# Finer load and store transfers, spread-out second statistics and shared buffers in a diagonal-LSTM and quantum-circuit kernel

## The chip, the cores and the metric

The kernel runs on one core of a Trainium2 chip. The metric is the device time of one execution in microseconds, the median of several runs. The core has five engines with queues of their own: PE (TensorE, matrix products; PEld is its weight load), DVE (VectorE), ACT (ScalarE), POOL (GpSimd) and SP (SyncE, which here only starts DMA transfers). Sixteen DMA engines move data between HBM and the on-chip SBUF, which all transfers share.

## The reference, cut to what matters

The input is 16 images of 128 channels and 64 x 64 pixels (33.5 MB in fp32). Layer 0 normalises, runs an LSTM along the diagonals of each image, and adds the result to its input. Layer 1 normalises that sum and applies, at every pixel, a small simulated quantum circuit, and adds again.

```python
def _gn(v, G=32, eps=1e-5):
    g = v.reshape(B_, G, C_ // G, H_, W_)
    m = jnp.mean(g, axis=(2, 3, 4), keepdims=True)
    s = jnp.var(g, axis=(2, 3, 4), keepdims=True)
    return ((g - m) / jnp.sqrt(s + eps)).reshape(v.shape)
...
x = x + _L0_conv_ref(_gn(x), L0_conv_w_is, L0_conv_b_is, L0_conv_w_ss, L0_conv_b_ss)
x = x + _L1_conv_ref(_gn(x), L1_conv_pre_w, L1_conv_pre_b, L1_conv_q_weights, L1_conv_post_w, L1_conv_post_b)
```

Each `_gn` needs the mean and the variance of a whole group (4 channels of one image, all pixels) before any pixel of layer 1 can be computed. The second `_gn` is therefore a barrier: its statistics are complete only after the last diagonal of layer 0.

## The kernel before, in words

**Stage 1, loading (0 to about 107 us).** All 16 images stream in. 40 of an image's 64 rows go into a resident buffer, `ring` (`rows(b)`, L230: for image 0 five pieces of 256 KB, for the others one piece of 1 MB and one of 256 KB). The other 24 rows are loaded only for statistics into rotating buffers (`behind(b)`, L239, three pieces of 256 KB, seven buffers). DVE takes `bn_stats` of every 128x512 piece (L263) in the order: ring rows of image b+1, then the rest of image b, then `bn_aggr` (L266). SP issues the loads in that same order. Beside this PE, ACT and POOL run 33 small recurrence steps (`inv_step`, L177 to L188), and `keep` (L332) issues products whose result nobody reads. After the last image come the group mean (`group_mean`, L137), the variance (L403 to L409) and `inverse_root` (L144 to L148), which gives `rstd1`; then POOL normalises the first diagonals (L546 to L556) and PE makes the first gates (L565).

**Stage 2, the scan (about 107 to 1290 us).** `NSTEP` = 160 diagonal steps. PE multiplies the hidden state (L694) and the next input (L565), ACT applies the gate functions (L713, L767), DVE forms the cell and hidden states (L757 to L776), POOL normalises the diagonal two steps ahead and adds the new hidden state onto the ring (`residual`, L599). Rows come finished in 16 groups of four rows (g = 0 to 15); `residual` appends the 16 images of a finished group to `waiting`, and in every step `statistics(n)` takes 4 or 6 of them with `bn_stats` over 128x256 (L651). After group 9 (`FIRST` = 10) a first sum is made (`early_sums`). The first 24 rows are written out to a DRAM scratch tensor, `low` (L605), and the rows that were left behind in stage 1 are loaded in their place (L655).

**The turn (1290 to 1303 us).** After the loop: `residual` of the last step, the `bn_stats` still waiting, then five DVE passes over the statistics of the last six groups (L619 to L631), the group sums on PE (L810), the variance (L811 to L815), `inverse_root`, and from `rstd2` and `mean2` the per-image weights `w_image` (L823) and offsets `b_image` (L832, with a product on PE, L831).

**Stage 3, the circuit (1303 to 1445 us).** Per image b: `angles` (theta, L865, 16 matmul records per image in the profile), `sines` (ACT L879, DVE L881 and L882, ACT L885), `squares` (PE L893, ACT L905), `outputs` (PE L911, in two halves of four 128x512 tiles) and `finish` (DVE L928: eight additions of 128x512 per image, result written over x1). Three of the eight chunks of an image lie in `low` and are loaded back by POOL (`load`, L854, 256 KB each, 14 buffers); the other five are in the ring. Stores: each low chunk alone (L930, 256 KB), and the ring rows by halves (L933: one chunk in the first half, four chunks as 1 MB in the second). A low buffer is free for the next load when its store has landed. The order on PE is outputs(b, 0), squares(b+1), outputs(b, 1), angles(b+3), so an `angles` that waits for a load also holds back the outputs behind it. All stages lie in a manual order: each engine works through its instructions as the program emits them.

Of the kernel before, what the change touches and what calls it, by code (L numbers as in the profile page):

```python
# [16 lines left out]
P = 128  # L17
# [11 lines left out]
FIRST = 10  # L29
# [50 lines left out]
def kernel(  # L80
# [28 lines left out]
    NLOW = NH - RING  # L109
    low = dram.tile([NB, P, NLOW * NW], F32, name="low")  # L110

# [9 lines left out]
    NG2 = NH // 4  # L121
    w_theta = const.tile([P, 128], F32, name="w_theta")
# [28 lines left out]
    with ExitStack() as scan:  # L151
# [16 lines left out]

        def inv_step(j, pool):
# [28 lines left out]
        with ExitStack() as prep:  # L198
            pp = prep.enter_context(tc.tile_pool(name="prep", bufs=1))
            rest_pool = prep.enter_context(tc.tile_pool(name="rest", bufs=7))  # L200
# [6 lines left out]
            ws_n = [rest_pool.tile([P, 2, 2 * P], F32, name=f"ws_n{i}", tag="rest") for i in range(2)]  # L207
            sum_n = rest_pool.tile([P, 4, P], F32, name="sum_n", tag="rest")
            wx_n = rest_pool.tile([P, 4, P], F32, name="wx_n", tag="rest")
# [14 lines left out]
            pieces = [(1, 5), (0, 1)]  # L224
            rests = {}

            def rows(b):
                for k0, k1 in ((1, 2), (2, 3), (3, 4), (4, 5), (0, 1)) if b == 0 else pieces:
                    at = (2 * k0 * ROWS - AHEAD) * NW if k0 else SLOTS * NW
                    nc.sync.dma_start(  # L230
                        out=ring[:, 2 * k0 : 2 * k1, b, :],
                        in_=xv[b, :, at : at + (k1 - k0) * CHUNK].rearrange("c (k n) -> c k n", n=BLOCK),
                    )

            def behind(b):
                rests[b] = []
                for k in range(RING * NW, NH * NW, CHUNK):
                    rest = rest_pool.tile([P, CHUNK], F32, name=f"rest{b}_{k}", tag="rest")
                    nc.sync.dma_start(out=rest, in_=xv[b, :, k : k + CHUNK])  # L239
                    rests[b].append(rest)  # L240
# [88 lines left out]
            def keep(pool, tag, v):  # L329

                ps = pool.tile([P, v.shape[-1]], F32, name=nc.get_next_instruction_name(), tag=tag)
                nc.tensor.matmul(ps, lhsT=ident, rhs=v, start=True, stop=True)  # L332

# [28 lines left out]
            for b in range(NB):  # L362
                if b + 2 < NB:
                    rows(b + 2)
                if b + 1 < NB:
                    behind(b + 1)
                    for k in (1, 2, 3, 4, 0):
                        statistics(b + 1, k)
                for k in (5, 6, 7):
                    statistics(b, k)  # L370
                aggregated(b)
                while b < NB - 1 and done * (NB - 1) < EARLY * (b + 1):
# [5 lines left out]
                    done += 1  # L378
            prep_ps.close()
# [18 lines left out]
            for v in (ring[:, 2, NB - 1, :], rests[NB - 1][0], rests[NB - 1][1]):  # L398
                keep(ps_small, "small", v)
# [5 lines left out]
            nc.vector.tensor_add(var, var, mv1[:, :, 1])  # L405
            ps = ps_small.tile([P, NB], F32, name="gv1", tag="small")
            nc.tensor.matmul(ps, lhsT=group, rhs=var, start=True, stop=True)
            keep(ps_gate, "gate", wxT)
            nc.vector.tensor_scalar_add(var, ps, EPS)  # L409
# [73 lines left out]
        dst = [work.tile([P, 2, NC], F32, name=f"diff{i}") for i in range(2)]  # L483
        edge = work.tile([P, NW, NB], F32, name="edge")
# [97 lines left out]
        def differences(t, now, diff):  # L582
            a, b = columns(t)
            nc.vector.tensor_sub(diff[:, 1, a:b], now[:, 1, a:b], now[:, 0, a:b])
            if a == 0:
                above = edge[:, t - BAND, :] if BAND <= t < BAND + NW else none
                nc.gpsimd.tensor_sub(diff[:, 0, 0:NB], above, now[:, 0, 0:NB])
# [4 lines left out]
        def residual(t, new):  # L592
# [8 lines left out]
            for g in range(NG2):  # L601
                if t == 4 * g + 3 + (NW - 1 if 4 * g < SLOTS else BAND + NW - 1 - SLOTS):
                    waiting.extend((g, i) for i in range(NB))
# [7 lines left out]

        parts = stats.rearrange("p b g (h s) -> p b (g h) s", s=3)
        moments = small.tile([P, 2, NB], F32, name="moments", tag="moments")
        more = small.tile([P, 2, NB], F32, name="more", tag="moments")

        def squared(k0, k1):

            dev = parts[:, :, k0:k1, 1]
            nc.vector.tensor_mul(dev, dev, dev)  # L619
            yield  # L620
            nc.vector.scalar_tensor_tensor(
                dev, parts[:, :, k0:k1, 2], 2.0 / BLOCK, dev, ALU.mult, ALU.add
            )
            yield

        def less_mean(k0, k1):
            dev = parts[:, :, k0:k1, 1]
            nc.vector.tensor_sub(dev, dev, mean2.unsqueeze(2).to_broadcast([P, NB, k1 - k0]))

        def total(to, k0, k1):  # L630
            nc.vector.reduce_sum(to, parts[:, :, k0:k1, 1], axis=mybir.AxisListType.X)  # L631

        def early_sums():
            k = 2 * FIRST
            total(moments[:, 0], 0, k)
            yield
            group_mean(ps_small, moments[:, 0], mean2, 2, 1.0 / k)
            less_mean(0, k)
            yield
            total(moments[:, 0], 0, k)  # L640
            yield
            yield from squared(0, k)
            total(moments[:, 1], 0, k)
# [3 lines left out]
        def statistics(n):  # L647
            for _ in range(min(len(waiting), n)):
# [3 lines left out]
                if (g, i) == (FIRST - 1, NB - 1):  # L652
                    sums.append(early_sums())
                if i == NB - 1 and 4 * g < NLOW:
# [30 lines left out]
        def step(t, ps):  # L685
# [42 lines left out]
            for later in sums:  # L728
                next(later, None)
# [3 lines left out]
            if t + 2 < NSTEP:  # L733
                normalised(t + 2)
            both = {}
# [49 lines left out]
            if t in (2, 3):  # L785
                nc.vector.memset(dst[t % 2], 0.0)
            if SLOTS - 1 <= t < SLOTS - 1 + NW:
                nc.gpsimd.tensor_copy(edge[:, t - SLOTS + 1, :], one_slot(new, SLOTS - 1))  # L788
            return later

# [3 lines left out]
        with tc.manual_schedule():  # L794
# [5 lines left out]
            residual(NSTEP - 1, hst[NSTEP % 2])  # L800
            statistics(len(waiting))
            k, n = 2 * FIRST, 2 * NG2
            less_mean(k, n)
            total(more[:, 0], k, n)
            for _ in squared(k, n):
                pass
            total(more[:, 1], k, n)
            nc.vector.tensor_add(moments, moments, more)
            ps = ps_small.tile([P, 2, NB], F32, name="gm3", tag="small")
            nc.tensor.matmul(ps, lhsT=group, rhs=moments, start=True, stop=True)  # L810
            nc.vector.tensor_scalar_mul(moments, ps, 1.0 / n)  # L811
            var = small.tile([P, NB], F32, name="var2", tag="gn_var")
            nc.vector.tensor_mul(var, moments[:, 0], moments[:, 0])
            nc.vector.tensor_sub(var, moments[:, 1], var)
            nc.vector.tensor_scalar_add(var, var, EPS)  # L815
            inverse_root(small, var, rstd2, 2)
            nc.vector.tensor_add(mean2, mean2, moments[:, 0])

            warm = small.tile([P, 1], F32, name="warm", tag="inv_t")
            nc.scalar.activation(warm, shift, AF.Sin)  # L820


        nc.vector.tensor_mul(  # L823
            w_image[:, :, 16:32],
            w_theta[:, 0:16].unsqueeze(1).to_broadcast([P, NB, 16]),
            rstd2.unsqueeze(2).to_broadcast([P, NB, 16]),
        )
        mr = small.tile([P, NB], F32, name="mr", tag="gn_var")
        nc.vector.tensor_mul(mr, mean2, rstd2)
# [174 lines left out]
```

## Time and profile before

| what | us |
|---|---|
| median of 3 runs | 1448.32 (1445.94 to 1449.99) |
| the profiled execution, its own time | 1447.33 |
| its span | 1445.3 |
| PE busy | 1364.7 (94%) |
| DVE busy | 972.1 (67%) |
| POOL busy | 897.7 (62%) |
| ACT busy | 764.1 (53%) |

The time of the profiled execution is 2.0 us more than its span, the stretch from the first to the last instruction. The shares of the busy time are averages over three stages that have different limits, so they say little about the two ends of the program. The row of the DMA engines' busy share does say something: in 40 slices of 36 us it stands at 9 tenths or more in the first two, at 8 or 9 in the last four, at nearly nothing in most of the slices between, and at 1 to 4 tenths in slices 17 to 22, where finished rows go out and the rows left behind come in.

### The profile page before, as it was taken

The numbers are of one execution on the slowest core, as the hardware profiler recorded it, in microseconds if no ns is written. First come the engines' busy times: TensorE is split into PE (matmuls) and PEld (weight loads), VectorE is DVE, ScalarE is ACT, GpSimd is POOL, SyncE is SP. The second block draws the span as 40 slices with busy tenths as digits, with TensorE's granted clock in tenths as the row PEclk, the third lists the DMA queues.
The fourth block names the chain that finished last, engine by engine and source line by source line (L and its number), as shares of the span: only waits on it lengthen the run. The fifth ranks groups of instructions, "written<-read, shape, count | busy, mean of one in ns | idle before, by whom it ended". The sixth has DMA issues, their size and how long they took to land. (4 is left out here: it accounts for less than half of the span.)

```text
span 1445.3 us, 19732 instructions
## 1 busy us (share of the span) xinstructions
PE 1364.7 (94%) x5942; PEld 964.2 (67%) x5942; DVE 972.1 (67%) x2450; ACT 764.1 (53%) x1855; POOL 897.7 (62%) x1717
## 2 busy tenths in 40 slices
PE   6778999999999999999999999999999998868887
PEld 5648887776677766677766777667776787853222
DVE  6884566566665666887777765555555588776786
ACT  5645665555555555555555555555555565533231
POOL 4215777776677777788887776666766676622210
PEclk9999999999999999999999999999999999999997
DMA  9970000000000000133444000000000000008998
GB/s 327 362 267 2 1 1 1 1 0 1 1 0 1 1 0 1 59 117 122 131 134 134 6 0 1 1 1 1 1 1 0 1 1 1 1 1 284 347 361 288
DMA packets 86008, 107.00 MB, mean 74 GB/s; under 512 B 3936, under 2 KB 70528, under 8 KB 85904
## 3 DMA queue, kind: packets, MB, share of 16 engines
q1 hardware_dynamic: 80624, 92.29, 18.9%
q0 software_dynamic: 4048, 12.67, 2.6%
q8 instruction: 47, 0.77, 0.2%
q10 hardware_dynamic: 1232, 0.80, 0.2%
q14 instruction: 57, 0.47, 0.1%
HBM read 59.61 MB, written 46.14 MB: 73 GB/s over the span
## 5 line engine op out<-in xcount | busy, mean ns | idle before, releaser
L565 PE MATMUL ps<-xn,wxT 128*128 128x512 f32 (+18 forms) x1280 | 481.3, 519 | 1.5 <-POOL xn L556 0.9
L709 DVE TENSOR_TENSOR ps<-ps,both 128x256 f32<-128x256 f32 (+9 forms) x544 | 219.2, 408 | 318.0 <-PE ps L694 311.6
L713 ACT ACTIVATE ps<-ps,bias 128x512 f32<-128x512 f32 (+23 forms) x480 | 268.3, 581 | 254.2 <-DVE ps L709 217.8
L565 PEld LDWEIGHTS ps<-xn,wxT 128*128 128x128 f32 x1280 | 232.3, 192 | 174.9 <-issue 155.6
L739 ACT COPY both<-ps 128x256 f32<-128x256 f32 (+9 forms) x544 | 191.4, 355 | 179.9 <-PE ps L694 160.2
L694 PE MATMUL ps<-diff,w0T 128*128 128x256 f32 (+14 forms) x1088 | 283.3, 363 | 0.0
L694 PE MATMUL ps<-diff,w1T 128*128 128x256 f32 (+14 forms) x1088 | 283.3, 362 | 0.0
L599 POOL TENSOR_TENSOR ring<-ring,hst 128x256 f32<-128x256 f32 (+8 forms) x488 | 247.8, 539 | 24.4 <-DVE hst L776 24.4
L694 PEld LDWEIGHTS ps<-hst,wsT 128*128 128x128 f32 x1088 | 195.9, 190 | 87.7 <-DVE hst L776 39.1
L694 PE MATMUL ps<-hst,wsT 128*128 128x256 f32 (+14 forms) x1088 | 241.4, 365 | 7.6 <-DVE hst L776 6.2
L694 PEld LDWEIGHTS ps<-diff,w0T 128*128 128x128 f32 x1088 | 199.8, 190 | 21.0
L694 PEld LDWEIGHTS ps<-diff,w1T 128*128 128x128 f32 x1088 | 199.8, 190 | 21.0
L556 POOL TENSOR_TENSOR xn<-xn,rstd 128x512 f32<-128x512 f32 (+10 forms) x160 | 170.8, 1067 | 14.8 <-DVE rstd L148 2.3
L551 POOL TENSOR_TENSOR xn<-ring 128x256 f32<-128x256 f32 (+8 forms) x213 | 146.8, 699 | 0.0
L776 DVE TENSOR_TENSOR hst<-g,ps 128x256 f32<-128x256 f32 (+13 forms) x320 | 107.8, 368 | 46.6 <-ACT g L767 44.1
L546 POOL TENSOR_TENSOR xn<-ring,mean 128x16 f32<-128x16 f32 (+8 forms) x247 | 130.4, 537 | 11.4 <-DVE mean L138 10.4
L767 ACT ACTIVATE g<-cst 128x256 f32<-128x256 f32 (+20 forms) x320 | 102.9, 368 | 64.6 <-DVE cst L766 64.0
L590 POOL TENSOR_TENSOR diff<-hst 128x240 f32<-128x240 f32 (+9 forms) x136 | 102.9, 756 | 40.8 <-DVE hst L776 37.0
L788 POOL COPY edge<-hst 128x16 f32<-128x16 f32 x64 | 25.1, 392 | 134.2 <-DVE hst L776 134.2
L766 DVE TENSOR_TENSOR cst<-cst,ps 128x256 f32<-128x256 f32 (+20 forms) x320 | 104.5, 368 | 5.5
L763 DVE TENSOR_TENSOR ps<-ps,g 128x512 f32<-128x512 f32 (+20 forms) x160 | 95.0, 594 | 18.3 <-ACT g L713 17.2
L713 ACT ACTIVATE g<-ps,bias 128x512 f32<-128x512 f32 (+20 forms) x160 | 97.3, 608 | 11.0 <-PE ps L694 3.3
(309 smaller groups left out, 1209.4 us busy)
## 6 DMA issues: line engine op xcount, KB each, us to landing
out_dram<-ring SPq DMA_DIRECT2D x16, 1024.0 KB, 6.0
ring<-in_x_dram SPq DMA_DIRECT2D x15, 1024.0 KB, 10.1
rest<-in_x_dram SPq DMA_DIRECT2D x48, 256.0 KB, 7.8
low<-ring SPq DMA_DIRECT2D x6, 2048.0 KB, 7.6
ring<-in_x_dram SPq DMA_DIRECT2D x6, 2048.0 KB, 8.0
low<-low POOLq DMA_DIRECT2D x48, 256.0 KB, 5.9
out_dram<-low SPq DMA_DIRECT2D x48, 256.0 KB, 4.6
ring<-in_x_dram SPq DMA_DIRECT2D x20, 256.0 KB, 10.1
```

Of the source, the lines that this page charges most:

```text
L546: nc.gpsimd.tensor_sub(by_pairs(xn, 0, j, n), x0, over(mean1, n))
L551: nc.gpsimd.tensor_sub(by_pairs(xn, 1, j, n), lower, of)
L556: nc.gpsimd.tensor_mul(v, v, r)
L565: nc.tensor.matmul(ps[g][:, :, a:b], lhsT=wxT[:, g * 128 : (g + 1) * 128], rhs=xns[t % 2][:, :, a:b], start=t > 0, stop=True, skip_group_c ...
L590: nc.gpsimd.tensor_sub(diff[:, 0, a1:b], now[:, 1, a1 - NB : b - NB], now[:, 0, a1:b])
L599: nc.gpsimd.tensor_add(x1, x1, by_pairs(new, q, j, n))
L694: nc.tensor.matmul(out, lhsT=w[:, g * 128 : (g + 1) * 128], rhs=rhs, start=False, stop=True, skip_group_check=True,)
L709: nc.vector.tensor_add(v, v, both[g][:, a:b])
L713: nc.scalar.activation(to[:, :, a:w], ps[g][:, :, a:w], FUNC[g], bias=bias[:, g : g + 1])
L739: nc.scalar.copy(both[g][:, a:b], ps[g][:, 0, a:b])
L766: nc.vector.tensor_add(c[:, q], c[:, q], ig[:, q])
L776: nc.vector.tensor_mul(new[:, q, a:v], th[:, q, a:v], act[GO][:, q, a:v])
```

## The change

What it does, part by part:

- **Loads in stage 1.** Every image's ring rows come in five pieces of 256 KB. Four of the seven buffers of `behind` are now fixed tiles, `spare`, which also hold the raw weights before, and serve as `diff` and `edge` in the scan and as four of the 14 low buffers in stage 3. The recurrence steps of an iteration are emitted ahead of its loads.
- **First statistics.** `keep` takes `wsT` for its weights and the rest pieces of the last two images for its data, and two more `keep` products stand around the variance's group sum.
- **Second statistics.** `early_sums` follows after group 7 (`FIRST` = 8). For each of groups 8 to 14, POOL subtracts the early mean, squares, and adds to running sums (`late_sums`, four operations). The last four images of group 14 and the last five of group 15 aren't taken by `bn_stats` on DVE but by two activations each on ACT (`by_scalar`, Identity and Square with a sum along the row). At the end PE adds all parts in one accumulator (`add`), with five `keep` products among them.
- **The turn.** ACT's Sqrt table is loaded by a one-column activation ahead; `w_image` is written for image 0 first, the others after.
- **Low loads.** Chunks 0 to 3 are loaded by SP at step 152 into the spare tiles. Later loads are emitted after `finish(b, 0)` instead of at the head of the iteration.
- **Stores.** Every chunk is stored alone, 256 KB, right after its addition.

```diff
-FIRST = 10
+FIRST = 8
+LATE = 4
...
+    spare = [const.tile([P, CHUNK], F32, name=f"spare{i}") for i in range(4)]
...
+            ORDERED = (1, 2, 3, 4, 0)
...
             def rows(b):
-                for k0, k1 in ((1, 2), (2, 3), (3, 4), (4, 5), (0, 1)) if b == 0 else pieces:
+                for k in ORDERED:
...
-            for v in (ring[:, 2, NB - 1, :], rests[NB - 1][0], rests[NB - 1][1]):
-                keep(ps_small, "small", v)
+            for v in (rests[NB - 2][0], rests[NB - 2][2], rests[NB - 1][0]):
+                keep(ps_small, "small", v[:, 0 : 3 * P])
...
+            keep(ps_gate, "gate", wxT[:, 0 : 3 * P])
             ps = ps_small.tile([P, NB], F32, name="gv1", tag="small")
             nc.tensor.matmul(ps, lhsT=group, rhs=var, start=True, stop=True)
             keep(ps_gate, "gate", wxT)
+            keep(ps_gate, "gate", wxT[:, 0:P])
...
-                    waiting.extend((g, i) for i in range(NB))
+                    n = {NG2 - 2: NB - LATE, NG2 - 1: NB - LATE - 1}.get(g, NB)
+                    waiting.extend((g, i) for i in range(n))
...
+        def deviations(engine, g, n):
+            d = dev[:, :, 0:n]
+            m = mean2[:, 0:n].unsqueeze(2).to_broadcast([P, n, 2])
+            engine.tensor_sub(d[:, 0], parts[:, 0:n, 2 * g : 2 * g + 2, 1], m)
+            engine.tensor_mul(d[:, 1], d[:, 0], d[:, 0])
+
+        def late_sums(g, n):
+            deviations(nc.gpsimd, g, n)
+            v = added[:, :, 0:n]
+            nc.gpsimd.tensor_add(v, v, dev[:, :, 0:n])
+            v = inner[:, 0:n]
+            nc.gpsimd.tensor_add(v, v, parts[:, 0:n, 2 * g : 2 * g + 2, 2])
+            yield
+
+        def by_scalar(g, i):
+            x1 = ring[:, block(4 * g), i, :]
+            for k, f in enumerate((AF.Identity, AF.Square)):
+                to = work.tile([P, BLOCK], F32, name=f"none{g}_{i}_{k}", tag=f"both{k}")
+                nc.scalar.activation(
+                    to, x1, f, bias=less[:, i : i + 1], accum_out=sums_of[:, g % 2, k, i : i + 1]
+                )
...
+            if t >= NSTEP - LATE:
+                by_scalar(NG2 - 2, NB - NSTEP + t)
+            if t == NSTEP - 8:
+                for n in range(4):
+                    low_rows(nc.sync, n, spare[n])
...
+            warm = small.tile([P, 1], F32, name="warm", tag="inv_t")
+            nc.scalar.activation(warm, shift, AF.Sqrt)
             residual(NSTEP - 1, hst[NSTEP % 2])
...
+            g, n = NG2 - 1, NB - LATE - 1
+            for i in range(n, NB):
+                by_scalar(g, i)
...
+            add(ps, by_half, moments, True)
+            for h in range(2):
+                add(ps, by_half, added[:, :, :, h])
+                add(ps[:, 1], by_one, inner[:, :, h])
+            add(ps, by_one, sums_of[:, 0])
+            for _ in range(3):
+                keep(ps_gate, "gate", wxT)
             statistics(len(waiting))
-            k, n = 2 * FIRST, 2 * NG2
-            less_mean(k, n)
-            total(more[:, 0], k, n)
-            for _ in squared(k, n):
-                pass
-            total(more[:, 1], k, n)
-            nc.vector.tensor_add(moments, moments, more)
...
+            deviations(nc.vector, g, n)
+            for h in range(2):
+                add(ps[:, 1, 0:n], by_one, parts[:, 0:n, 2 * g + h, 2])
+            add(ps, by_one, sums_of[:, 1])
+            for h in range(2):
+                add(ps[:, :, 0:n], by_half, dev[:, :, 0:n, h])
...
+            nc.vector.tensor_copy(m, ps[:, 0])
+            nc.vector.scalar_tensor_tensor(var, m, -1.0, m, ALU.mult, ALU.mult)
+            nc.vector.scalar_tensor_tensor(var, var, EPS, ps[:, 1], ALU.add, ALU.add)
+            for _ in range(2):
+                keep(ps_gate, "gate", wxT)
             inverse_root(small, var, rstd2, 2)
...
+            image_weights(0, 1)
+            nc.vector.tensor_add(mean2, mean2, m)
+            mr = small.tile([P, NB], F32, name="mr", tag="gn_var")
+            nc.vector.tensor_mul(mr, mean2, rstd2)
+            image_weights(1, NB)
...
-    lowp = ctx.enter_context(tc.tile_pool(name="lowp", bufs=14))
+    lowp = ctx.enter_context(tc.tile_pool(name="lowp", bufs=10))
...
             nc.vector.scalar_tensor_tensor(x1, y, b_out, x1, ALU.add, ALU.add)
-            if k < NT:
-                nc.sync.dma_start(out=ov[b, :, k * CHUNK : (k + 1) * CHUNK], in_=x1)
-        for r0, r1 in (((NLOW, SLOTS),), ((SLOTS, NH),))[h]:
-            q = block(r0)
-            nc.sync.dma_start(
-                out=ov[b, :, r0 * NW : r1 * NW].rearrange("c (k n) -> c k n", n=BLOCK),
-                in_=ring[:, q : q + (r1 - r0) // ROWS, b, :],
-            )
+            o = ov[b, :, k * CHUNK : (k + 1) * CHUNK]
+            nc.sync.dma_start(out=o if k < NT else o.rearrange("c (k n) -> c k n", n=BLOCK), in_=x1)
...
-            if b + 4 < NB:
-                load(b + 4)
             po = outputs(b, 0)
             later = sines(b + 2) if 0 < b < NB - 2 else iter(())
             finish(b, 0, po)
+            for n in range(NBUF + NT * b, min(NBUF + NT * b + NT, NT * NB)):
+                load(n)
```

## The prediction

> **What bounds the kernel now.** I read the strip of 40 slices first. PE stands at 9 through the scan, and DMA at 8 or 9 in the first three and the last four slices: the scan belongs to PE, both ends to transfers, or to what starts and ends them. The change hardly touches PE's work in the scan, so the time must come from the ends. There I read three views: the timeline of stage 1's end, the timeline of the turn, and busy time by stretches.
>
> The end of stage 1 (start us, us, engine, line, operation, count, idle time before):
>
> ```profile
> 95.80 3.06 DVE L263 BATCH_NORM_STATS2 stats<-ring 128x6 f32<-128x512 f32 x5 [0.55 <-DMA ring<-in_x_dram]
> 98.78 1.86 DVE L263 BATCH_NORM_STATS2 stats<-rest 128x6 f32<-128x512 f32 x3
> 100.97 1.81 DVE L263 BATCH_NORM_STATS2 stats<-rest 128x6 f32<-128x512 f32 x3
> 102.81 0.37 DVE L266 BATCH_NORM_AGGREGATE mv<-stats 128x2 f32<-128x48 f32 x1
> ```
>
> DVE waits until 95.80 for the last image's 1 MB piece, then owes eleven statistics at once and ends at 103.18. The stretches from 99.5 on show that the loads have ended by 100.0 (45 GB/s in the last half, then 0). So DVE runs 3.2 us behind the data.
>
> The turn, from the timeline:
>
> ```profile
> 1289.79 6.62 DVE L651 BATCH_NORM_STATS2 stats<-ring 128x6 f32<-128x256 f32 x20
> 1298.97 0.64 PE L810 MATMUL gm<-moments,wide_sb 128*128 128x32 f32 x2 [10.11 <-DVE moments L808]
> 1299.42 6.03 POOL L854 DMA_DIRECT2D low<-low  x11 [9.24 <-DVE moments L808]
> 1303.33 2.01 PE L865 MATMUL theta<-ring,w_image 128*32 128x512 f32 x4 [0.36 <-DVE b_image L832]
> 1308.36 0.69 ACT L879 ACTIVATE y<-theta,b_image 128x512 f32<-128x512 f32 x1 [5.99 <-PE theta L865]
> 1310.94 1.13 PE L893 MATMUL am<-y,w_amp 64*128 64x512 f32 x4 [1.06 <-ACT y L885]
> 1314.75 1.59 SPq L930 DMA_DIRECT2D out_dram<-low  x3
> ```
>
> Twenty `bn_stats` and five passes on DVE hold everything; no low load starts before 1299.42 and no store before 1314.75. The stretches after it:
>
> ```profile
> core 0: us, PE busy (x) PEld busy (x) DVE busy (x) ACT busy (x) POOL busy (x), PEclk, DMA share, GB/s
> 1289.60:1299.40 9.80, 0.42 (x2) 0.43 (x2) 9.12 (x28) 1.28 (x1) 0.23 (x1) 0.73 0.00 1
> 1299.40:1303.30 3.90, 0.82 (x3) 0.58 (x4) 2.35 (x12) 1.70 (x3) 3.79 (x7) 0.50 0.60 193
> 1303.30:1314.75 11.45, 9.68 (x48) 3.38 (x48) 3.08 (x6) 3.50 (x6) 3.76 (x8) 0.80 0.70 255
> 1314.75:1330.00 15.25, 15.25 (x86) 5.03 (x84) 12.71 (x21) 5.38 (x9) 3.22 (x6) 1.00 0.81 262
> 1330.00:1415.00 85.00, 76.81 (x373) 24.79 (x372) 66.50 (x106) 25.11 (x42) 15.09 (x28) 0.98 1.02 358
> 1415.00:1439.30 24.30, 21.84 (x74) 8.16 (x72) 20.38 (x31) 4.12 (x7) 0.00 (x0) 0.75 0.78 272
> 1439.30:1445.30 6.00, 0.00 (x0) 0.00 (x0) 0.01 (x1) 0.00 (x0) 0.00 (x0) 0.50 0.74 249
> ```
>
> For 85 us DMA is full at 358 GB/s, and PE and DVE wait for loads (theta starts again at 1342.4, 1359.6, 1384.6 and 1408.7 behind one). Around this lie ramps: 255 and 262 GB/s ahead, 272 and 249 behind. Free of waits an image takes 6.84 us (DVE's first additions at 1322.48, 1329.32, 1336.17). Stage 3 is a full DMA queue with two ramps.
>
> **Stage 1: -2.8 us.** Bytes and loading order stay. DVE's work per image is 3.06 + 1.86 + 0.37 = 5.3 us, against 5.8 us of loading (its waits recur at 90.00 and 95.80), so with pieces of 256 KB it can follow piece by piece: one statistic (0.67) and the aggregate (0.37) after the last landing near 99.9, 100.95 instead of 103.18: -2.2. SP's issue of a ring piece takes about 0.5 (four in 1.97 at the start), of a rest 0.48: 5 x 0.5 + 3 x 0.48 = 3.9 us per image, under 5.8. If that cover went, each 0.1 us over it would cost 1.5 us. The first sixteen gate products took 3.44 us at 106.77, where eight take 1.06 at full clock (1282.36): 1.3 us lost. The new `keep` products may hold the clock, or, run slowly (1.90 for 512 columns at 99.31, so 1.4 for 384), outlast the 0.90 gap ahead of `gv` by 0.5. Between -1.3 and +0.5 I take -0.6: the products of the last rests now end close to the group mean.
>
> **Scan: 0.** POOL gets 4 operations for each of 7 groups, at 0.25 (rows of 128x32): 1 us in a step, 7 in all, behind `normalised`. POOL works 62% of the span and waits for `hst` in most steps (134.2 us ahead of L788 alone), so they lie in that wait; uncovered they would cost up to 7. `early_sums` moves from narrow steps into wide ones, where PE is the bound: 0 to -2. In the last four steps ACT gets two 128x256 activations each, in a gap of 1.09 us (Tanh to the next gate, 1280.13 to 1281.22). A 128x256 COPY is 372 ns: 0.74, it fits. Sums along the row are shown by no row: 0.28 each if they overlap as the squares of 128x512 do (0.60 long, 0.50 apart), 0.60 if reading out the sum costs 0.2. At 0.60 each of three steps grows by 0.1. SP's four early loads pass nothing: its next instruction is the first store.
>
> **The turn up to the first store: -6.6 us.** DVE starts after `residual` (1290.18) and owes 11 statistics of 0.331: 1293.9; two operations on 128x22, 0.2 each: 1294.35. ACT: last Tanh at 1289.6, two activations to 1290.3, table 1.28 and warm-up 0.2 to 1291.8, ten activations of 0.37: **1295.5** (1294.6 at 0.28, 1297.8 at 0.60; I take the COPY, the nearest row). So ACT ends last. Behind it PE has three small products queued, 0.7: 1296.2. DVE three operations, ACT root 0.25, DVE four and `w_image` of one image: 3 x 0.22 + 0.3 + 0.9 + 0.2, so theta can start at 1298.3; the two `keep` of 1.06 queued ahead of it on PE end at 1298.4. Gain here: 4.9.
>
> Here a rule is weighed. The Trainium skill (TensorE: Matmul & The Clock Gate, Part 1) has PE fall to half clock after an idle window of about 3.4 us. The row shows 0.73, then 0.50, behind PE's end at 1288.9. The three `keep` can start when POOL's last `late_sums` is done, 1291.2, after 2.3 us of idling: by the rule at full clock, done by 1294.5, theta(0) then taking its 1.85. Read from the row alone, which has no products in the gap, they could run at half (2.1 each), end at 1297.7 and push the sum back 1.5, and theta to 3.5. I take the rule.
>
> theta(0) needs chunks 0 to 2, loaded already: 1300.3 (before 1308.2, with half clock and waits). theta(1), queued ahead of am(0), needs chunk 5. The low pool lies on memory of the scan, whose last reader is the second `keep`: loads from 1298.4 + 0.5; the trace has at least 3.5 us to landing, so chunk 5 is there at 1302.9 and theta(1) done at 1304.3. That holds am(0), whose sine would be ready at 1302.8: 1.5 us remain of a wait that was hidden before. From am to the first store 3.8 us as before (1310.94 to 1314.75): **1308.1**, against 1314.75. If the loads needn't wait for the `keep`, 1306.6; with slow sums or half clock, 1310.6.
>
> **The ramp: -2.7 us.** Before, the four ring chunks of the second half wait for each other and go as 1 MB (L933, two issues in 3.02 us), and DMA stands nearly still at 1319 to 1320 and 1328 to 1330 (24 to 58 GB/s). At 262 against 358 GB/s, 15.25 us lose 4.1 us of transfer. Stored one by one, an image needs 2.1 MB of stores and 0.79 of loads, 8.05 us at 358 for 6.84 us of production, so the queue can stay full once loads flow: I take two thirds. As the 85 us behind it are full, what is moved earlier is gained.
>
> Here a rule speaks against the change: the skill (DMA: Bandwidth & Descriptors, Measured) asks for at least 1 MiB per transfer, with 341 GB/s there and 138 at 64 KB. For 256 KB I estimate 240 from that page, halfway. The trace disagrees where small pieces stand together: 1323 to 1327, mostly single chunks, moved 387 to 400 GB/s a microsecond. By the rule 32.5 MB (15 pieces of 1 MB in stage 1, 16 in stage 3) would cost 135 us instead of 91, +44; by the row nothing. I take the row, since several pieces are in flight at once.
>
> **The full queue and the end: -1.8 us.** The same 42.5 MB follow the first store, and 14 low chunks precede it in both. Loads wait for the same stores; on POOL's queue nothing else stands. The last four images run free of loads with PE at 0.75 clock, unchanged. The last 1 MB store was issued at 1439.3 and landed at 1443.7: 4.4 us. A 256 KB store with little ahead of it lands in 2.1 (1314.75), with some queue 2.6: -1.8.
>
> **Sum:** -2.8 - 6.6 - 2.7 - 1.8 = -13.9, from the profiled 1447.33 to 1433.4; its run is 1.0 under the median shown, so **1434.4**, own range 1429 to 1439.
>
> **The rivals.**
> - *Bytes rule stage 3.* If the first load's start counts and use of the queue stays as it was (46.1 MB in 145.9 us, 316 GB/s), the gain is 0.5 us of start, 1.05 MB / 316 = 3.3, and stage 1's 2.8: **1441.7**. For: share 1.02 for 85 us. Against: DMA stood at 0 at 1313 to 1315, waiting for the first store.
> - *Production becomes the bound.* Load waits vanish: from 1308.1 on 16 x 6.84 + 1.7 (first image) + 2.5 (slow clock at the end) + 4.2 = 117.9, with stage 1 a span of 1423.2: **1426.3**. This needs 373 GB/s throughout; single stretches reach 390, the mean is 358.
> - *Small pieces slow the queue.* In stage 1 and in stage 3's stores; slower than before as soon as the 32.5 MB fall under 310 GB/s (105 us for 91); at 240, **1478**.
> - *The change doesn't do what it says:* ACT's sums at 0.60, cold `keep` products, loads late, each wait replaced by the next: stage 1 and the tail remain, less a microsecond of POOL: about **1445**.
>
> **The numbers.** Chances: forecast 0.68, bytes 0.14, production 0.10, no change 0.04, slow pieces 0.04. The range 1426 to 1442 takes in the first three. A measurement of this kernel tells about 0.3% (4.3 us) from no change; so faster 0.92, same 0.04, slower 0.04.
>
> **What would show it.** Stage 1's last aggregate at 101 rather than 103.2. ACT's row with sums: 0.37 or 0.6. theta(0) 8.5 us after the last `hst` (before 13.5), first store 18.2 us after it (before 24.9). No MB-sized holes in the first 15 us of stores, and the last landing some 2.5 us after DVE's last addition. Wrong it is if the stretch of full DMA drops under 340 GB/s, if SP issues stretch stage 1, or if steps of the scan grow.

## The result, and the profile after

| | before | after |
|---|---|---|
| median, us | 1448.28 (1445.40 to 1449.99, 8 runs) | 1438.88 (1434.39 to 1443.61, 8 runs) |
| profiled execution, its own time | 1447.33 | 1438.96 |
| its span | 1445.3 | 1437.1 |

The ratio is 0.9936, with a 95% interval of 0.9918 to 0.9955: faster by 9.4 us, where 13.9 had been forecast. The time lies inside the forecast range. The four stages don't agree with their forecasts as well as the sum does. The table cuts the span at three events that both traces have: the start of the first `hst`, the end of the last one, and the issue of the first store. The column of the forecast has the prediction's own terms.

| stretch of the span | before | after | difference | forecast |
|---|---|---|---|---|
| start of the span to the first `hst` | 109.69 | 114.21 | **+4.5** | -2.8 |
| first `hst` to the end of the last (the scan) | 1180.18 | 1177.68 | **-2.5** | 0 |
| end of the last `hst` to the first store | 24.88 | 19.81 | **-5.1** | -6.6 |
| first store to the end | 130.57 | 125.39 | **-5.2** | -4.5 |
| sum | 1445.3 | 1437.1 | -8.2 | -13.9 |

So the gain came from the turn and from stage 3, about as forecast, and from the scan, where none was expected; stage 1, which was to give 2.8 us, took 4.5.

The end of stage 1 after, from DVE's timeline (start, us, engine, line, operation, count):

```profile
104.50 1.82 DVE L276 BATCH_NORM_STATS2 stats<-spare 128x6 f32<-128x512 f32 x3
106.35 0.37 DVE L279 BATCH_NORM_AGGREGATE mv<-stats 128x2 f32<-128x48 f32 x1
```

The last aggregate ends at 106.72 instead of the 103.18 of before, or the 100.95 of the forecast.

The turn after, from the timeline of all engines (idle time before an instruction, and what ended it, in brackets):

```profile
1292.24 3.69 DVE L691 BATCH_NORM_STATS2 stats<-ring 128x6 f32<-128x256 f32 x11 [0.34 <-POOL ring L611]
...
1298.45 0.49 ACT L681 ACTIVATE none<-ring,less 128x256 f32<-128x256 f32 x1
1298.85 0.19 ACT L681 ACTIVATION_READ_ACCUMULATOR none<-ring,less 128x1 f32 x1
1299.09 0.41 PE L868 MATMUL gm<-sums_of,by_one 128*128 128x32 f32 x2 [1.67 <-ACT none L681]
...
1302.08 0.71 PE L946 MATMUL theta<-ring,w_image 128*32 128x512 f32 x2 [0.34 <-DVE mean L904]
...
1302.37 5.40 POOL L844 DMA_DIRECT2D low<-low  x10 [9.11 <-ACT warm L893]
...
1306.11 0.62 PE L946 MATMUL theta<-low,w_image 128*32 128x512 f32 x1 [0.68 <-DMA low<-low]
...
1311.70 0.34 SPq L1011 DMA_DIRECT2D out_dram<-spare  x1
```

DVE has done its eleven statistics at 1295.9. ACT, with a pair of entries for each activation (the activation, then the read of its sum), ends at 1299.04, and PE waited 1.67 us for it. The last `hst` ended at 1291.89, so theta(0) starts 10.2 us after it (before 13.5) and the first store is issued 19.8 after it (before 24.9).

Stage 3 after, busy time by stretches (columns as in the forecast: the stretch, its length, busy us of PE, PEld, DVE, ACT and POOL, the PE clock, the DMA share, GB/s):

```profile
1311.70:1327.00 15.30, 15.30 (x86) 5.03 (x84) 12.76 (x20) 5.38 (x9) 3.21 (x6) 1.00 0.91 311
1327.00:1407.00 80.00, 76.22 (x367) 24.23 (x367) 64.70 (x103) 24.46 (x41) 15.08 (x28) 0.98 1.03 366
1407.00:1432.00 25.00, 23.39 (x80) 8.69 (x78) 21.02 (x33) 4.78 (x9) 0.00 (x0) 0.80 0.83 295
1432.00:1437.10 5.10, 0.43 (x1) 0.00 (x0) 1.22 (x2) 0.00 (x0) 0.00 (x0) 0.50 0.72 241
```

The first stretch moves 311 GB/s (before 262), the full one 366 (358), the one behind it 295 (272). From the end of DVE's last addition to the end of the span it is 3.9 us instead of 6.0.

### Where stage 1 lost its time

Busy time by stretches shows a hole in the loads, 20 to 24 us after the start (the last column is GB/s):

```profile
20.00:22.00 2.00, 2.00 (x10) 1.77 (x9) 0.76 (x2) 1.50 (x5) 0.52 (x3) 1.00 0.00 0
22.00:24.00 2.00, 1.94 (x17) 1.88 (x16) 0.00 (x0) 1.30 (x6) 0.05 (x1) 1.00 0.02 7
```

The timeline of SP's queue shows the stop: five ring pieces up to 14.80, and the next load only at 22.95.

```profile
10.99 3.81 SPq L239 DMA_DIRECT2D ring<-in_x_dram  x5
22.95 1.29 SPq L252 DMA_DIRECT2D spare<-in_x_dram  x3
```

The list of SP's waits from 8 to 40 us (waited for, us in all, times, longest) names what it waited for:

```profile
SPq L252 <- PE w1T_ps L314: 8.1, 1, 8.1
```

L314 is the transposition of the raw weights on PE; its last group, `w1T`, runs from 22.5, and by 22.9 it has read the first tile. The fixed order `(3 * b + i) % 7` gives image 1 the numbers 3, 4 and 5, which are `spare[0]` to `spare[2]`, and these still hold raw weights or their sums. All later loads stand behind this one on SP's queue.

### The profile page after: what moved, and what is told of

It reads as the page before. It is cut to its first block, busy times and chain, and to the rows that moved or that the text cites. A ratio compares the mean times of both kernels' runs of the same rounds, so it can differ in the third digit from the quotient of the medians.

```text
span 1437.1 us, 19999 instructions
## 1 busy us (share of the span) xinstructions
PE 1374.7 (96%) x5976; PEld 971.0 (68%) x5976; DVE 973.1 (68%) x2437; ACT 773.7 (54%) x1892; POOL 903.8 (63%) x1747
## 5 line engine op out<-in xcount | busy, mean ns | idle before, releaser
L737 PE MATMUL ps<-spare,w1T 128*128 128x256 f32 (+14 forms) x1088 | 283.4, 363 | 0.0
L737 PE MATMUL ps<-spare,w0T 128*128 128x256 f32 (+14 forms) x1088 | 283.3, 362 | 0.0
L737 PEld LDWEIGHTS ps<-spare,w0T 128*128 128x128 f32 x1088 | 199.9, 190 | 20.9
L737 PEld LDWEIGHTS ps<-spare,w1T 128*128 128x128 f32 x1088 | 199.8, 190 | 20.9
L602 POOL TENSOR_TENSOR spare<-hst 128x240 f32<-128x240 f32 (+9 forms) x136 | 102.9, 757 | 35.7 <-DVE hst L821 31.9
L839 POOL COPY spare<-hst 128x16 f32<-128x16 f32 x64 | 25.1, 392 | 134.3 <-DVE hst L821 134.3
```

What stands on the lines that cost most here:

```text
L737: nc.tensor.matmul(out, lhsT=w[:, g * 128 : (g + 1) * 128], rhs=rhs, start=False, stop=True, skip_group_check=True,)
```

## The experiments

Each kernel ran beside the kernel before on its own chip; a ratio is to that one. `e12_after_again`, the changed kernel unaltered, is the yardstick.

> The changed kernel unaltered, as the yardstick for the other runs on one chip. Ratio to the kernel before 0.9936 as measured, between 0.992 and 0.9955.

Measured: 1439.31 us, ratio 0.9920 [0.9906, 0.9935]; the hole in the loads is there again (222 GB/s from 20 to 30 us). It agrees with the 0.9936 above. One thing differs in its profile, with the same program: in the turn PE's clock falls to half for 3.4 us (the value behind POOL's busy time), where the profile above has 1.00 throughout.

```profile
1292.93:1296.34 3.41, 3.41 (x8) 1.86 (x8) 2.27 (x8) 3.41 (x15) 0.00 (x0) 0.50 0.00 0
```

### Stage 1: the order of the tiles, and small pieces

`e1_rotation` alters only which tile a rest of the first two images gets, so that none is asked for before its weights are read:

```diff
-                    n = (3 * b + i) % 7
+                    n = 3 * b + i
+                    n = (0, 1, 2, 5, 6, 0)[n] if n < 6 else (n - 5) % 7
```

> The changed kernel with one thing altered: which of the seven rest buffers the three pieces of image 1 use (the sum of the weights' tile, the input weights' tile and the first piece of image 0 again, instead of the two raw state weights and the sum). My theory: stage 1 lost its gain because SP's loads for image 1 wait for the last transposes of the raw weights, and the DMA engines stand still from 19 to 24 us. Then the hole goes, the last aggregate ends near 101.5 us instead of 106.7, and the time falls by 5 us to about 1433.5. Rival: pieces of 256 KB with at most eight in flight load more slowly; then the last aggregate stays above 105 and the time within 1 us of the changed kernel's.

Measured: 1433.08 us, ratio 0.9875 [0.9843, 0.9906]. A stretch and DVE's timeline of this kernel:

```profile
20.00:30.00 10.00, 8.81 (x60) 7.09 (x58) 9.80 (x17) 7.11 (x36) 2.29 (x12) 1.00 1.08 370
```

```profile
99.94 0.37 DVE L280 BATCH_NORM_AGGREGATE mv<-stats 128x2 f32<-128x48 f32 x1
```

The hole is gone (370 GB/s where the changed kernel has 166 in the same ten microseconds), the last aggregate ends at 100.31 and the first `hst` starts at 107.23: 7.0 us earlier than in the changed kernel and 2.5 earlier than before. Everything behind it keeps its length (turn 19.93, first store to end 125.2). One line of tile numbers was worth 7 us of the profile; by the ratios (0.9875 against 0.9920 and 0.9936) it was 6.5 to 9 us.

From the last aggregate to the first `hst` it is 6.9 us here and was 6.5 before, although the first sixteen gate products ran faster. The two timelines show what took the time, the kernel before and then `e1_rotation`:

```profile
106.46 0.25 POOL L556 TENSOR_TENSOR xn<-xn,rstd 128x32 f32<-128x32 f32 x1 [2.29 <-DVE rstd L148]
106.77 3.44 PE L565 MATMUL ps<-xn,wxT 128*128 128x128 f32 x16 [0.87 <-POOL xn L556]
```

```profile
104.00 0.53 POOL L638 TENSOR_SCALAR by_one<-wide_sb 128x128 f32<-128x128 f32 x1
104.61 0.25 POOL L569 TENSOR_TENSOR xn<-xn,rstd 128x32 f32<-128x32 f32 x1
104.91 2.05 PE L578 MATMUL ps<-xn,wxT 128*128 128x128 f32 x16 [1.68 <-POOL xn L569]
```

The change lets POOL clear three tiles (L636) and scale a matrix (L638) for the second statistics, and these stand on POOL's queue ahead of the first `xn`: it starts 1.2 us after `rstd` instead of 0.15. That is 1.0 us, of which the faster products give back 0.6. No run moved these operations elsewhere.

`e2_big_pieces` is `e1_rotation` with the ring rows of images 1 to 15 as before, 1 MB and 256 KB; `e7_small_before` is the kernel before with the small pieces only, on its own pool of seven buffers:

```diff
-            pieces = [(1, 5), (0, 1)]
+            pieces = [(1, 2), (2, 3), (3, 4), (4, 5), (0, 1)]
```

> The same buffers as e1_rotation, but the ring rows of images 1 to 15 come as one piece of 1 MB and one of 256 KB, as before. If the small pieces do what I forecast, DVE again owes eleven statistics after the last 1 MB piece, and the last aggregate ends 2 us later than in e1_rotation (about 103.5); if small pieces cost transfer rate, it ends earlier than there, and the time is lower.

> The kernel before with one thing altered: the ring rows of all images in pieces of 256 KB. If small pieces let DVE follow the loads, as forecast, the last aggregate ends near 101 us instead of 103.2, and nothing else moves: about 2 us less than before. If small pieces slow the queue in stage 1, it ends later than 103.2.

Measured: `e2_big_pieces` 1436.18 us, 0.9901 [0.9864, 0.9938]; its last aggregate ends at 101.80, 1.5 later than in `e1_rotation`, its first `hst` 1.8 later. The intervals of the two ratios overlap. `e7_small_before` 1449.73 us, 0.9995 [0.9985, 1.0004]; last aggregate 102.72, only 0.5 earlier than before.

Two things have to be told apart here: when the last bytes arrive, and how long DVE works after that. The stretches show the last bytes, in the kernel before and then in `e7_small_before` (the next half microsecond has 0 GB/s in both):

```profile
99.50:100.00 0.50, 0.50 (x1) 0.13 (x1) 0.50 (x2) 0.00 (x0) 0.00 (x0) 0.50 0.12 45
```

```profile
100.50:101.00 0.50, 0.50 (x1) 0.23 (x2) 0.50 (x2) 0.00 (x0) 0.00 (x0) 0.50 0.07 25
```

With big pieces DVE's last aggregate ends 3.2 us after the loads (before) and 3.3 us after them (`e2_big_pieces`, whose loads end by 98.5); with small pieces it ends 1.7 us (`e7_small_before`) and 1.8 us after them (`e1_rotation`, also by 98.5). So the small pieces save 1.5 us in both pairs. In `e7_small_before` most of this doesn't show, because its loads ended 1 us later than before. The loads moved 359 GB/s from 30 to 90 us there and 362 before, 369 in `e1_rotation` and 371 in `e2_big_pieces`; one profile each doesn't settle whether small pieces cost this 1%.

DVE's timeline in `e7_small_before` looks at first as if the statistics had become slower:

```profile
94.71 3.43 DVE L263 BATCH_NORM_STATS2 stats<-ring 128x6 f32<-128x512 f32 x5
98.13 2.05 DVE L263 BATCH_NORM_STATS2 stats<-rest 128x6 f32<-128x512 f32 x3
100.50 1.82 DVE L263 BATCH_NORM_STATS2 stats<-rest 128x6 f32<-128x512 f32 x3
```

Five statistics took 3.06 before and take 3.43 here, three took 1.86 and take 2.05; the last three, with their loads landed, take 1.82. The longer rows hold short waits for the pieces. In the trace two of the pieces behind the second row land at 98.78 and 99.46, and their statistics start at 98.81 and 99.49. From 40 to 98 us 40 of 80 statistics start within 0.06 us of a recorded landing, before only 8 of 80. The gaps are so short that the list of waits shows none of them. So DVE follows the loads piece by piece, as the prediction had it, and 5.85 us per image (3.43 + 2.05 + 0.37) is the pace of the loads, not DVE's own.

### The scan: where the early sum stands

`e8_first8_before` is the kernel before with `FIRST = 8`; `e6_first10` is the changed kernel with `FIRST = 10`.

> The kernel before with one number altered: the early sum after group 7 instead of group 9 (FIRST = 8). Theory A: the 2.5 us that the scan gained come from moving this sum from narrow steps near 140 to wide ones near 104: first to last hst falls from 1180.2 to about 1178, and the turn grows by about 0.5 us, as DVE's five passes now take 16 parts instead of 12. Theory B: the gain comes from the spreading of the statistics onto POOL and ACT: first to last hst stays at 1180.2.

> The changed kernel with FIRST = 10 as before, so that the early sum runs after group 9, in narrow steps, and POOL's running sums take groups 10 to 14. My theory: the 2.5 us that the scan gained came from moving the seven DVE passes of the early sum out of steps 140 to 144 into steps where PE is the bound. Then the stretch from the first to the last hst is 2 to 2.8 us longer than the changed kernel's 1177.7. Rival: it came from where the sum stands within a step (behind the statistics instead of ahead of them); then the stretch stays at 1177.7.

Measured: `e8_first8_before` has 1177.6 us from the first to the last `hst`, where the kernel before has 1180.2. Step by step against the kernel before, the ends of the steps stand as follows:

```
after step    96    104    136    140    141    142    143    145    159
late by us  +0.31  +0.53  +0.53  +0.54  -1.36  -1.86  -2.29  -2.55  -2.53
```

The sum costs 0.2 us in the wide steps at 104 and saves 3.1 in steps 140 to 145. That is all of the 2.5 us that the changed kernel's scan gained. The turn of `e8_first8_before` is 0.5 longer (first store 25.40 after the last `hst`), and its one run of 1448.19 us, against a median of 1450.37 before on that chip, is within the scatter. `e6_first10` goes the same way: 1179.3 us for the scan instead of 1177.7 (one run, 1439.09 us). That is 1.6 longer, less than the 2 to 2.8 expected: 0.9 us of the kernel before is saved at step 141 although the sum still stands there. Another part of the change does that, perhaps the sum's place within its step; no run tests it alone.

### The turn: ACT's sums, the kept products, the early loads

`e5_three_rot` is `e1_rotation` with three instead of five images of group 15 on ACT (the other two on DVE). `e9_const_keep` is that with the two last `keep` products reading `group` and `spare[3]` instead of `wxT`, which lies under the low pool.

> e1_rotation with three images of the last group on ACT instead of five, and 13 instead of 11 on DVE. An image costs ACT 0.98 us (two activations that end in a read of the sum) and DVE 0.335. My theory: ACT is what the turn waits for; ACT then ends 5.1 us after the last hst instead of 7.05, DVE's statistics at the same time, and theta and the first store come 1.8 us earlier, the time 1.8 us below e1_rotation. If DVE or PE were what it waits for, theta stays at 10.2 us after the last hst.

> e5_three_rot with the two kept products behind the group sums taken from tiles outside the low pool's memory (the group matrix and a spare tile). e4_no_keep showed both that the low loads wait for these products and that without them the clock falls. So here the first low load starts some 2 us earlier relative to theta, theta(1) no longer waits for chunk 5, the clock stays, and the first store comes 1 us earlier than in e5_three_rot (about 17 us after the last hst). If the loads wait for something else as well, nothing changes against e5_three_rot.

Measured, after the last `hst`: with five images ACT's last activation ends at 7.05 (the read of its sum at 7.15), theta(0) starts at 10.2 and the first store is at 19.8; with three 5.08, 8.35 and 17.98; with the other `keep` also, the first low load starts at 6.2 instead of 8.6 and the first store is at 17.31. So ACT's activations did hold the turn, and the `keep` products did hold the loads. The totals don't show it: 1433.68 us, 0.9875 [0.9858, 0.9891], and 1432.44 us, 0.9871 [0.9855, 0.9888], against 0.9875 of `e1_rotation`. An interval of 0.0016 to either side is 2.4 us, about the size of the gain, so whether stage 3 gives it back isn't settled. In the single profiles it does: from the first store to the end it is 125.2 us in `e1_rotation`, 126.2 in `e5_three_rot` and 128.1 in `e9_const_keep`.

`e4_no_keep` is the changed kernel without these two products.

> The changed kernel without the two products kept behind the group sums. If the low loads wait for them (they read a tile that lies under the low pool), the first load starts 1.8 us earlier (8.6 instead of 10.4 us after the last hst), chunk 5 lands before theta(1) needs it, and the first store comes 1 us earlier. If the loads wait for the last activation or for DVE instead, they start at the same point. If the products hold the clock, theta(0) takes over 3 us instead of 2.3 and the first store comes later.

Measured: 1439.30 us, 0.9916 [0.9884, 0.9948]. The first low load starts 7.9 us after the last `hst` instead of 10.5, but the first store is at 21.2 instead of 19.8. The stretches show the clock:

```profile
1292.00:1295.00 3.00, 3.00 (x5) 1.20 (x4) 1.17 (x5) 3.00 (x13) 0.00 (x0) 0.58 0.01 3
1295.00:1298.00 3.00, 1.81 (x12) 1.35 (x10) 0.77 (x4) 1.43 (x6) 1.38 (x3) 0.99 0.02 3
1298.00:1301.00 3.00, 2.05 (x9) 0.42 (x9) 1.28 (x7) 1.19 (x2) 3.00 (x7) 0.50 0.91 284
1301.00:1304.00 3.00, 3.00 (x16) 1.04 (x18) 0.17 (x1) 0.35 (x1) 1.01 (x2) 0.50 0.99 354
```

Theta(0) and most of theta(1) ran at half clock. The first fall, at 1291, has nothing to do with the two products, which come later; `e12_after_again` has it at nearly the same place (2.1 us after the last `hst`, here 2.3). But `e12_after_again` has the products and no second fall, so they did hold the clock there. They cost the loads 2.6 us and bring the first store forward by 1.4.

They don't hold it in every execution. In `e6_first10`, with the same products, it fell in front of them (PE's timeline):

```profile
1299.29 2.06 PE L177 MATMUL I-10574_10575<-wxT,wsT 128*128 128x512 f32 x2
1301.13 1.72 PE L177 MATMUL I-10577_10578<-wxT,wsT 128*128 128x512 f32 x2
```

Two products took 2.06 and 1.72 us instead of 1.11 and 1.02, theta(0) began 11.6 us after the last `hst` instead of 10.2, and the first store was 1.7 later.

`e11_no_preload` is the changed kernel without SP's four loads at step 152, which POOL issues instead.

> The changed kernel without the four chunks loaded by SP at step 152; POOL loads them in the turn as it does the others. Theory A (the early loads are what let theta(0) start when w_image is ready): theta(0) waits for loads that start at 10.5 us after the last hst, and the first store comes 3 to 4 us later than 19.8 after it; the end follows by less, as stage 3 is bound by bytes. Theory B (the sums alone brought the turn's gain): first store at 19.8 us after the last hst as in the changed kernel.

Measured: 1443.81 us, one run. It doesn't answer its question: POOL issued them late in the scan, from 1242.2 on, when the scan's use of the spare tiles ends, and they landed long before the turn. The program emits them behind the scan, so at the border of two stages an engine's order is not always the order of emission. The first store came at 21.8, 2.0 later than in the changed kernel, but theta(0) waited for no load; the last two `keep` again took 2.06 and 1.68. What the early loads are worth was not measured.

### Stage 3: stores, and the clock at the end

`e3_halves` is the changed kernel with the ring rows stored by halves as before (four chunks as 1 MB).

> The changed kernel with the stores of stage 3 as before (low chunks alone, ring rows by halves, 1 MB in the second). My theory puts 4.5 us of gain on storing chunk by chunk (ramp 2.7, last store 1.8): first store to end 130 us instead of 125.4, the time about 1443. If the gain behind the first store came from the preloaded chunks or from scatter, it stays at 125 to 126 and the time at 1439.

Measured: 1445.11 us (20 runs), 0.9957 [0.9945, 0.9969]. Against the changed kernel's 0.9920 and 0.9936 the chunk stores are worth 0.0021 to 0.0037, that is 3 to 5 us; its interval lies apart from that of 0.9920 and overlaps with that of 0.9936. In its profiled execution, one of its slower ones, the stretch from the first store to the end is 134.4 us instead of 125.4, which overstates it. The ten profiles of kernels that store chunk by chunk have 123.5 to 128.7 us there, the four that store by halves 130.6 to 134.4.

`e10_tail` is `e9_const_keep` with two unread products of 128x512 for each of the images 13 and 14, in the place where no theta is left to compute.

```diff
+            elif b + 1 < NB:
+                idle = ps_t.tile([P, CHUNK], F32, name=f"idle{b}", tag="theta")
+                for _ in range(2):
+                    nc.tensor.matmul(
+                        idle, lhsT=w_theta, rhs=w_image.rearrange("p b c -> p (b c)")[:, 0:CHUNK], start=True, stop=True
+                    )
```

> The kernel e9 (rotation, three images on ACT, constant keep) plus two unread 128x512 products per image beside the outputs of the last images, where no theta is left to compute. Theory A: behind the last load PE runs at a granted clock of about 0.80 (1407 to 1432 us) because nothing fills its gaps, and the outputs (3.95 us for four halves instead of 1.1 to 1.9) make the tail; then the clock stands near 1.0 in the last 25 us and the end comes about 2 us earlier: 1430.5 against e9's 1432.4. Theory B (DVE's eight additions of 6.8 us per image set the pace of the tail): the clock rises and the time does not move, within 0.5 us of e9.

Measured: 1428.68 us (1428.13 to 1435.86, 5 runs), 0.9867 [0.9845, 0.9889]. From 1407 to DVE's last addition, `e9_const_keep` and then `e10_tail`:

```profile
1407.00:1425.90 18.90, 16.55 (x44) 6.81 (x40) 14.92 (x23) 2.38 (x5) 0.00 (x0) 0.61 0.83 294
```

```profile
1407.00:1421.90 14.90, 12.97 (x45) 4.68 (x44) 12.96 (x20) 1.71 (x3) 0.00 (x0) 1.00 0.88 309
```

The clock stands at 1.00 instead of 0.61. From the last addition of image 13 to that of image 15 it is 12.75 us instead of 14.85: the 2.1 us that were expected. Of the other profiles `e9_const_keep` is one of the slowest here: in all thirteen without the added products the clock stands at half for some of these two images, and they take 13.2 to 14.9 us, the changed kernel 14.4 and then 13.2 (`e12_after_again`). So the products save between 0.4 and 2.1 us, as the fall happens to lie. The profiled spans differ by 3.5, as `e10_tail` also took 2.6 us less from image 0 to image 12 (370 GB/s against 351, with the same transfers) and began the scan 1.0 later. The intervals of the two ratios overlap, so the gain is shown in the trace and not in the ratio. It has the lowest median of all, and it, like `e1_rotation`, `e5_three_rot` and `e9_const_keep`, lies below the changed kernel.

## Why the prediction came out as it did

**The sum** came nearer than its terms. Stage 1 missed by 7.3 us; the scan, put at 0, gave 2.5, which covered part of it. That the time lay inside the range is in part luck. With the fault of stage 1 mended (`e1_rotation`) the gain is 17.3 us on that chip, more than the 13.9 forecast.

**Stage 1 is the step that failed.** It said that bytes and loading order stay, and priced the loads by the time SP needs to issue them, "under 5.8". The order did stay; the tiles didn't. The pool of before gave out its buffers in the order in which they came free, and the fixed order asks for three that hold raw weights. I had named the double use of `spare` in the change, and gave it no price: 8.1 us of waiting on a queue in order. Without it (`e1_rotation`) the total comes close, aggregate 100.31 for 100.95, first `hst` 2.5 earlier than before for 2.8, but misses cancel in it. DVE follows the pieces as forecast, but this saves 1.5 us and not 2.2. The loads end 1.4 us earlier than before, which was put at nothing: in all five kernels without the hole they end between 98.5 and 99.3, in the three built on the kernel before between 99.9 and 101.0. Which part of the change does it was not tested. The clock gives the 0.6 that was forecast, and POOL's new operations ahead of the first `xn` take 1.0, for which there was no term. In the changed kernel itself the new `keep` products didn't hold the clock: it stood at half from 104.2 to 111.1.

That the small pieces slow the queue by anything near the third that 240 GB/s would mean is refuted for this kernel, and the rule of 1 MiB with it: 369 GB/s against 371 in one pair of kernels, 359 against 362 in the other (30 to 90 us). One reading was wrong without a consequence: the third of the 40 slices has 7 tenths of DMA, not 8 or 9.

**The scan** was put at 0 within 0 to -2, and gave 2.5. The mechanism was named, the moved early sum, and the value chosen was its wrong end: steps 140 to 145 had no cover for its passes on DVE, which the trace of before shows in its step times (step 141 took 7.8 us between steps of 5.8 and 6.2) and which I didn't read. POOL's additional sums cost nothing that can be seen.

**The turn** gave 5.1 of 6.6. Two terms were short. ACT's activation with a sum takes 0.49 us from start to start; I had taken 0.37, that of a COPY, and kept 0.60 as the far end. The COPY was the wrong row: an activation of 128x256 took 0.41 before (Tanh, L767), one of 128x512 with a bias per partition 0.69 (L879) and without it 0.60 (L905). This one has such a bias, and the read of its sum as a second entry. Its last activation ends 7.05 after the last `hst` instead of 5.6, and `e5_three_rot` shows that it was what PE waited for. The gain was also cut by theta(1), as forecast, behind loads that the `keep` hold back (0.68 of waiting). The rule of the clock, weighed against the row at half clock, gave the right value for this execution (granted 1.00 from 1292.2 to 1327), but by luck: in `e12_after_again` the same program fell to half after 2.1 us of idling, and two of the three `keep` products took 2.05 and 1.59 us. It cost nothing there, as ACT ended last.

**The ramp and the end** were put at -4.5 together and gave 5.2 in the profile; `e3_halves` puts the stores' share at 3 to 5 us. The tail was to shrink by 1.8 and shrank by 2.1. The slow clock of the last images had been seen and left as it is; `e10_tail` puts its price at up to 2.1 us.

**The rivals.** "No change" named slow sums, cold products and late loads as what might eat the gain. The first is about half true, the second was seen in two other builds and in `e12_after_again`, the third cost 0.68 us. That small pieces slow the queue is refuted. "Bytes rule stage 3" stays possible for what goes beyond the change: earlier first stores (`e5_three_rot`, `e9_const_keep`) moved no median.

## What to carry to other kernels

Where a pool that hands out buffers as they come free is replaced by fixed tiles, list for the first uses of each tile who reads its old content and when: a load queued in order behind one such reader stops all loads after it, here for 8.1 us. Ask the same of every new operation at the border of two stages: who stands behind it on its queue (POOL's cost 1.0 us here). A sum moved out of a stretch whose engine has no cover is gained, here 2.5 us, and step times of the old trace show the stretch. A row that has grown longer is not always slower work: compare its starts with the landings of what it reads. A queue of short products that nobody reads is worth its cost only where the clock would fall, and it must read nothing that a transfer waits to overwrite.

## What the hardware showed unasked

- An ACT activation of 128x256 with a sum along the row and a bias per partition takes two entries, 0.49 and 0.19 us, which overlap to one pair for every 0.49 us. The length of the first needs no price for the sum: Tanh of the same shape, without a bias, takes 0.41, and a bias makes 0.69 of 0.60 us at 128x512.
- `bn_stats` of 128x512 follow each other every 0.59 us when their data are there (kernel before, `e2_big_pieces`), though each row is 0.68 us long; when each waits for its own piece, as in `e7_small_before`, they are 0.69 apart.
- PE's clock fell to half after it had been busy for only part of a few microseconds, and came back 3.4 us later (`e6_first10`, from 1299.12 to 1302.53). In the 3.41 us ahead of the fall PE was busy for 1.75 us with a longest wait of 1.66 us; in `e12_after_again` for 1.33 us with 2.08; and in the last images of `e9_const_keep`, with products that use 32 rows of the array, for 2.72 us with 0.69. The same products met the fall at other places in other builds. The Trainium skill (TensorE: Matmul & The Clock Gate, Part 1) has the window run freely, so that one program can meet it at different phases; these traces agree, as the changed kernel fell in the turn in one execution and not in the other. Its condition of a whole idle window of about 3.4 us isn't what these three show.
- With the same transfers, the full stretch of stage 3 moved 351 GB/s in one profiled execution and 370 in another, 2.6 us from image 0 to image 12, as much as most edits here were worth, so one profile doesn't decide on stage 3. In the slower one PE's clock was at half for 6.8 us of the stretch; which of the two came first isn't shown.
